# Four graph layers on one core: the order of column chunks in the attention layers

## The chip, the cores and the metric

The kernel runs on one core of a Trainium2 chip. The metric is the device time of one execution in microseconds (us). A difference between two kernels is one of the medians of repeated runs.

## The reference

A graph of 2708 nodes has an adjacency of zeros and ones, about 16 neighbours a node, and features of 512 numbers. Four layers follow each other, each with a residual and a layer norm:

```python
x = layernorm(x + relu((a_norm @ x + x) @ W0 + b0))          # layer 0
x = layernorm(x + a_norm1 @ x @ W1.T + b1)                   # layer 1
# layer 2: two attention layers, then the norm
for W in W_stack:                                            # h is the input of the first
    Wh, Ws = split(h @ W, 2)
    a = softmax(Wh @ Ws.T, axis=-1) * adj
    h = leaky_relu(a @ Wh + h, 0.01)
x = layernorm(x + h)
x = layernorm(x + adj @ (x @ W3) + b3)                       # layer 3
```

The softmax goes over all 2708 nodes; only its products with the neighbours are used.

## The kernel before

The text calls the two attention layers "layer 0 and layer 1" of the attention, as the code does, and the other layers the graph layers 0, 1 and 3. Nodes are handled in 22 blocks of 128 rows, the last with 20. The columns of the adjacency's transpose are cut into six chunks, `CH`: four of 512, one of 384 (blocks 16 to 18) and one of 276 (blocks 19 to 21). Source blocks are grouped in `GROUPS`, of 4, 4, 4, 4, 3 and 3.

A graph layer runs over steps (chunk k, group g). In each, `multiply` adds the products of a group's rows with the group's bytes of the mask into four accumulators. Rows are split in a high and a low half (`halve`: ACT makes `xh`, DVE makes `xl`), so a product appears twice, as `acc<-m,xh` and `acc<-m,xl`. The mask bytes `at` are loaded two steps ahead on SP's queue (`load_bytes`), and ACT casts them into `m`.

An attention layer first projects (`project_steps`): `wst` per chunk, and `z` per block, which is written to a scratch tensor in memory, `pairs`, in two slots that chunks use in turn. Then `layer` takes the chunks one after the other:

- `scores`: 22 matmul groups (`sp<-xs,wst_sb`) fill a chunk's columns for all source blocks; ACT copies them to `s`, DVE keeps the greatest (`top`).
- `shift_rows` and `shift_columns` make the maximum of each column (`tr_top`, `tr_mx` on PE).
- `soften`: 22 tiles, each with a subtraction (`s<-s,shift`), an exponential on ACT, a running sum (`sum<-sum,s`) and a product with the mask (`s<-s,a`). SP stores the tile beside z's rows into `pairs`.
- `fetch`: POOL gathers from `pairs`, by lists of neighbours (`givers`), 12 indirect transfers for a full block, 3 for the block of 20 rows. So a chunk of 512 has 48, that of 384 has 36 and that of 276 has 27. Eleven buffers hold them.
- `weigh`: PE multiplies each gathered tile into the result (`acc<-g`), and `end` adds the residual (`xr<-acc,rden,xr`). In layer 1 it also gathers statistics, and `normalize` writes the rows that graph layer 3 starts from (`made`).

These stages overlap: while chunk k is scored, chunk k-1 is softened and gathered, and chunk k-2 is weighed. The order of instructions on every engine is written out when the program is built (class `Ordered`, whose line is 71 in all rows of the profile). A clock that is only modelled decides there where a weighing is placed (`advance`, `until`, and 1.15 us for a gather); on the chip each engine follows that order and waits on semaphores. What fills PE after the last scores is a generator: the projections of layer 1 (`second`) after layer 0, and the first steps of graph layer 3 (`early`) after layer 1.

`early` takes 12 steps, groups 0 to 3 of chunks 0 to 2. Ahead of a step it makes sure that the rows it needs exist. `need(i)` places all weighing that is still missing for block i, in order, whether its gathers are expected or not:

```python
if t < 2:
    self.attention.need(GROUPS[t + 2][1] - 1)    # blocks 8 to 11, then 12 to 15
...
if t == 4 * TWO - 1:                             # the twelfth step
    self.attention.need(GROUPS[4][1] - 1)        # blocks 16 to 18
```

Groups 4 and 5 of the first chunks follow after the attention is done. The functions that the change touches are these:

Of the kernel before, what the change touches and what calls it, by code (L numbers as in the profile page):

```python
# [19 lines left out]
P = 128  # L20
N = 2708
D = 512
# [3 lines left out]
BANK = 512  # L26

CH = [(0, 512), (512, 512), (1024, 512), (1536, 512), (2048, 384), (2432, 276)]

GROUPS = [(0, 4), (4, 8), (8, 12), (12, 16), (16, 19), (19, 22)]  # L30
GW = 256
# [484 lines left out]
class Fast:  # L516
# [17 lines left out]
    def run(self):  # L534
        kernel, nc = self.k, self.nc
        with ExitStack() as ctx:
            pool = lambda name, bufs, **kw: ctx.enter_context(
                self.tc.tile_pool(name=name, bufs=bufs, reuse_waits="tile", **kw)
            )
            self.pages, self.wides = pool("pages", PAGES), pool("wides", WIDES)  # L540
            self.small, self.lists = pool("small_f", 4), pool("lists", 1)
            self.banks = [pool(f"banks{h}", 4, space=PSUM) for h in range(2)]
            given = [kernel.x_in[bass.ts(i, P), :] for i in range(NB)]
            l0 = Layer(0, given, kernel.w0, kernel.b0)
            l1 = Layer(1, kernel.saved[0], kernel.w1, kernel.b1)
            l3 = Layer(3, kernel.saved[2], kernel.w3, kernel.b3)
            self.attention = attention = Attention(self)
            self.jobs, self.due, self.other, self.beats = [], None, 1, 0
            run = Run(l0, l1)
            for t in range(len(run.seq)):  # L550
                self.step(run, t)
            attention.project(attention.layers[0], 0)
            for g in range(3):
                self.ends(run, g)
                if g == 1:
                    attention.project(attention.layers[0], 1)


            run = Run(l3)
            run.seq = [(l3, k, g) for k in range(TWO) for g in range(4)]  # L560
            run.seq += [(l3, k, g) for g in (4, 5) for k in range(2)]
            run.seq += [(l3, k, g) for k in range(2, TWO) for g in (4, 5)]
            run.seq += [(l3, k, g) for k in range(TWO, len(CH)) for g in range(len(GROUPS))]
            attention.run(self.early(run))
            for j in range(*GROUPS[5]):
                l3.rows[j] = attention.made[j]
            for t in range(4 * TWO, len(run.seq)):
                self.step(run, t)

            ly, k = run.before  # L570
            parts = self.project(ly, k)
            for some in (parts[:-1], parts[-1:]):
                made = []
                for i, n, ps in some:
                    made.append((i, n, self.combine(ly, k, len(made), i, n, ps)))
                self.finish(ly, k, made)
# [185 lines left out]
    def load(self, ly, k, g):  # L762

        c0, cw = CH[k]
        if (k, g) in ly.loaded:
            return
        ly.loaded.add((k, g))
        js = range(*GROUPS[g])
        if ly.number == 0:
            tiles = []  # L770
            for j in js:
                if k == 0:
                    self.load_rows(ly, j)
                at = self.wide(f"at{ly.number}_{k}_{j}")
                tiles.append(at)
                if j < NB - 1:
                    self.nc.sync.dma_start(
                        at[:, :cw], self.k.adj_t[bass.ts(j, P), c0 : c0 + cw]
                    )
                    continue  # L780

                few = self.k.adj_t[j * P : j * P + QW, c0 : c0 + cw]
                for d in range(DC):
                    self.nc.sync.dma_start(at[d * QW : (d + 1) * QW, :cw], few)
            ly.done["at", k, g] = tiles
        else:
            self.load_bytes(ly, k, g)
        if k == 0 and ly.number == 3 and g < 4:
            for j in range(*GROUPS[g]):
                self.load_rows(ly, j)  # L790
        if ly.number == 0 and g == (2 if k else 4):
            xt = [self.page(f"xt{k}_{c}") for c in range(DC)]
            for c in range(DC):
                self.nc.gpsimd.dma_start(xt[c][:, :cw], self.k.x_t[:, c, c0 : c0 + cw])
            ly.done["xt", k] = xt
# [318 lines left out]
    def step(self, run, t):  # L1114

        ly, k, g = run.seq[t]
        self.other = (k + 1) % 2
        self.before_products(run, t)
        if ly.number == 0 and (k, g) == (1, 0):
            self.attention.blank()  # L1120
        if ly.number == 1 and k == len(CH) - 1 and g in (2, 3, 4):
            self.attention.begin(g - 2)
        self.multiply(ly, k, g)
        if g == len(GROUPS) - 1 and k in ly.begun:
            self.evict(ly, k)
        wide = CH[k][1] == BANK
        if run.before and run.phase in ((1, 3, 4, 5) if wide else (1, 5)):
            self.work("PE")
        if run.before:
            self.ends(run, run.phase)  # L1130
            run.phase += 1
            if run.phase in ((3, 4, 5) if wide else (4,)):
                self.work("DVE")
        if g == (4 if ly.number == 3 and k < TWO else 3):
            self.residual(ly, k)
        if g == len(GROUPS) - 1:
            if ly.number == 3:
                self.biased(ly, k)
            if ly.number == 0:
                ends = self.degree_ends(ly, k)  # L1140
                next(ends)
                if k == len(CH) - 1:
                    note = self.prepare(
                        *run.seq[t + 1], between=lambda: next(ends), late=True
                    )
                for _ in ends:
                    pass
            while run.before and run.phase < 2:
                self.ends(run, run.phase)
                run.phase += 1  # L1150
            if k in ly.acc:
                self.evict(ly, k)
            if ly.number == 0:
                self.checked()
            run.before, run.phase = (ly, k), 0
            if ly.number == 0 and k == len(CH) - 1:
                note()
                self.load_weights(run.layers[1])
            if ly.number == 1:
                self.jobs.append((k, self.index(k)))  # L1160
                self.work("DVE")
# [178 lines left out]
class Chunk:  # L1340


    def __init__(self, ly, k):
        self.ly, self.k, self.cw = ly, k, CH[k][1]
        self.name = f"{ly.number}_{k}"
        self.blocks = blocks_of(k)
        self.s, self.masks, self.ends = {}, {}, []
        self.softened = 0
        self.fetched, self.rden = [], None
# [17 lines left out]
class Attention:  # L1367
# [29 lines left out]
    def blank(self):  # L1397
# [3 lines left out]
        for pairs in (p for ly in self.pairs for p in ly):  # L1401
            self.nc.sync.dma_start(
                pairs[N:, : 2 * PAIR + D].rearrange("j (r d) -> j r d", d=D),
                t[:n, :].unsqueeze(1).to_broadcast([n, (2 * PAIR + D) // D, D]),
            )

    def begin(self, step):

# [196 lines left out]
    def soften(self, ch):  # L1605
# [2 lines left out]
        nc, v, cw = self.nc, ch.softened, ch.cw  # L1608
        ch.softened += 1
        if v < NB:  # L1610
            if v == 0 and ch.k >= 2:

                assert not self.chunks[ch.k - 2].to_fetch
            n = rows_of(v)
            s = ch.s[v][:n, :cw]
            nc.vector.tensor_sub(s, s, ch.shift[:n, :cw])
# [9 lines left out]
        else:  # L1626
            nc.vector.tensor_add(ch.sum[:n, :cw], ch.sum[:n, :cw], s)
        nc.vector.tensor_mul(s, s, ch.masks.pop(j)[:n, :cw])
        to = ch.ly.pairs[ch.k % 2][j * P : j * P + n, :]
        if cw == BANK:  # L1630
            nc.sync.dma_start(
                to[:, : 2 * PAIR].rearrange("j (r x) -> j r x", x=PAIR)[:, :, D:],
# [26 lines left out]
    def fetch(self, ch):  # L1659
# [5 lines left out]
        if q not in ch.x:  # L1665
# [9 lines left out]
        self.nc.gpsimd.indirect_dma_start(  # L1675
            out=g[:, :width],
            out_offset=None,
            in_=ch.ly.pairs[ch.k % 2][:, :],
            in_offset=bass.IndirectOffsetOnAxis(ap=self.k.givers[:, i, t : t + 1], axis=0),
            element_offset=(q // 2) * PAIR + first,  # L1680
        )
# [103 lines left out]
    def run(self, next_layer):  # L1785

        f = self.f
        f.other = 1
        chunks = [[Chunk(ly, k) for k in range(len(CH))] for ly in self.layers]
        for k in range(2, len(CH)):  # L1790
            self.load_xt(self.layers[0], k)
            self.load_xt(self.layers[0], k + 1)
# [8 lines left out]
    def layer(self, ly, chunks, fill):  # L1801
        f = self.f
        self.chunks, self.made = chunks, {}
        for k, ch in enumerate(chunks):
# [4 lines left out]
            for n, j in enumerate(js):  # L1809
# [9 lines left out]
                self.scores(ch, j)  # L1819
                f.beat()  # L1820
                if n == 14 and k:
                    f.packed(k - 1)
                if n == 4 and k + 1 < len(chunks):
                    self.load_moving(chunks[k + 1])
                if k + 1 == len(chunks) and n in ((5, 11, 19) if ly.number == 0 else (5, 11)):
# [24 lines left out]
        done = self.clock + (2 if ly.number == 0 else 4)  # L1850
        while last.softened <= NB:
            self.soften(last)
            done += 1.4
            self.until(done, fill)
        while any(c.to_weigh for c in chunks):
            if not self.weigh() and not next(fill, False):
# [19 lines left out]
    def second(self, first):  # L1876
# [4 lines left out]
        yield True  # L1881
        self.load_w(ly)
        yield True
        self.load_xt(ly, 0)
        yield True
        yield from mixing
        for k in range(len(CH)):
            if k + 1 == len(CH) - 1:
                while self.pending:
                    self.pending.pop(0)[1]()  # L1890
                self.load_moving(first)
            if k + 1 < len(CH):
                self.load_xt(ly, k + 1)
            yield from self.project_steps(ly, k)


# [63 lines left out]
```

## Time and profile before

| | |
|---|---|
| time, median of 3 runs | 2307.89 us (2305.75 to 2312.35) |
| the profiled execution: time, and its span | 2333.96 us, 2332.2 us |
| busy PE, DVE, POOL, ACT | 2281.0, 1408.7, 705.9, 675.3 us |
| gathers (`g<-pairs,givers`) | 510, 1029 ns each on POOL |
| scores (`sp<-xs,wst_sb`, 512 columns) | 1344 matmuls of 594 ns |
| early and other products of graph layers, 512 columns | 1008 with `xh`, 1008 with `xl`, of 405 and 394 ns |
| DMA | 486.34 MB, mean 209 GB/s |

The profile is one execution, with times from the start of the span. Matmuls are pipelined, so the duration of one is longer than the distance between two: products of 512 columns start 0.23 us apart, matmuls of 512 columns in f32 are two passes in the trace. A row of a timeline has its start, its duration, the engine and line, the operation with the tiles it writes and reads, and in brackets the engine's idle time before it with what ended it. The word `issue` means that the profile shows no releaser.

### The profile page before, as it was taken

What the parts mean: (1) busy time and instruction counts of PE and PEld (TensorE: products, weight loads), DVE (VectorE), ACT (ScalarE), POOL (GpSimd) and SP (SyncE); (2) the same over time, 40 slices, a digit from 0 to 9 for tenths busy, and PEclk for the clock granted to TensorE, in tenths of its full rate; (3) what the DMA queues carried; (4) which work ended last, traced back from release to release, by engine and by line L of the source; (5) the groups of instructions that cost most, each with busy time, mean ns of one, the idle gap of its engine ahead of it and who ended that gap; (6) DMA issues with size and microseconds to landing.
All of it is one profiled execution on the core that took longest, in us unless ns stands there. A gap on an engine that the chain in (4) does not pass through costs nothing.

```text
span 2332.2 us, 25904 instructions
## 1 busy us (share of the span) xinstructions
PE 2281.0 (98%) x8525; PEld 1291.3 (55%) x8525; DVE 1408.7 (60%) x2803; ACT 675.3 (29%) x1354; POOL 705.9 (30%) x822
## 2 busy tenths in 40 slices
PE   9999999999999999999999999999999998899997
PEld 6676777777645444343555444444343454466685
DVE  6777886787554446857666511247868777534523
ACT  7444352222111123222222200123233233342221
POOL 3333431111000002534556540001634556442000
PEclk9999999999999999999999999999999999999999
DMA  9966752223557314867879997314867889873311
GB/s 349 283 186 185 186 169 79 75 79 103 205 200 267 119 45 167 309 203 276 282 268 375 326 411 301 143 41 175 291 208 270 295 284 360 270 225 117 121 50 43
DMA packets 260929, 486.34 MB, mean 209 GB/s; under 512 B 40238, under 2 KB 126950, under 8 KB 260784
## 3 DMA queue, kind: packets, MB, share of 16 engines
q1 hardware_dynamic: 192128, 269.63, 33.2%
q0 software_dynamic: 68656, 214.96, 28.2%
q8 instruction: 69, 1.13, 0.2%
q14 instruction: 76, 0.62, 0.1%
HBM read 307.55 MB, written 176.92 MB: 208 GB/s over the span
## 4 chain that ended last, share of the span: by engine, by line
PE 83%; DVE 6%; DMA 4%; issue 3%; POOL 1%; ACT 1%; another core or an unknown queue 1%; SPq 0%; POOLq 0%; DVEq 0%; ACTq 0%
PE sp L71 30%; PE acc L71 29%; PE mm L71 8%; PE z L71 6%; PE wst L71 6%; DMA g<-pairs,givers 1%; POOL g L71 1%; DVE s L71 1%; DMA at<-in_adj_t 1%; DMA x<-in_x 1%; DVE sum L71 1%; PE mix L71 1%; PE list L71 1%; PE tr_x2b L71 1%
## 5 line engine op out<-in xcount | busy, mean ns | idle before, releaser
L71 PE MATMUL sp<-xs,wst_sb 128*128 128x512 f32 (+3 forms) x2112 | 798.6, 545 | 0.4 <-issue 0.4
L71 POOL DMA_INDIRECT g<-pairs,givers x510 | 525.0, 1029 | 897.7 <-issue 399.7
L71 PEld LDWEIGHTS sp<-xs,wst_sb 128*128 128x128 f32 (+1 forms) x2112 | 379.6, 186 | 409.1 <-issue 341.8
L71 PE MATMUL acc<-m,xh 128*128 128x512 f32 (+4 forms) x1584 | 569.1, 381 | 8.4 <-ACT m L71 5.9
L71 PE MATMUL acc<-m,xl 128*128 128x512 f32 (+4 forms) x1584 | 552.1, 366 | 13.4 <-issue 10.9
L71 PEld LDWEIGHTS acc<-m,xh 128*128 128x128 f32 (+1 forms) x1584 | 289.3, 189 | 74.7 <-issue 23.6
L71 PEld LDWEIGHTS acc<-m,xl 128*128 128x128 f32 (+1 forms) x1584 | 289.6, 189 | 59.3 <-issue 17.2
L71 PE MATMUL acc<-g 128*32 128x512 f32 (+1 forms) x1020 | 268.2, 606 | 6.9 <-DMA g<-pairs,givers 3.5
L71 ACT ACTIVATE s<-s 128x512 f32<-128x512 f32 (+3 forms) x264 | 151.8, 580 | 339.6 <-DVE s L71 213.6
L71 ACT COPY s<-sp 128x512 f32<-128x512 f32 (+2 forms) x252 | 132.2, 527 | 392.8 <-PE sp L71 298.1
L71 DVE TENSOR_TENSOR top<-top,s 128x512 f32<-128x512 f32 (+2 forms) x240 | 149.4, 622 | 155.8 <-ACT s L71 123.3
L71 PE MATMUL mm<-w,ht 128*128 128x512 f32 (+1 forms) x528 | 225.0, 594 | 4.0 <-DVE ht L71 4.0
L71 ACT CAST m<-at 128x512 fp32r<-128x512 uint8 (+5 forms) x396 | 199.6, 567 | 70.0 <-DVE r L71 14.5
L71 DVE TENSOR_TENSOR s<-s,shift 128x512 f32<-128x512 f32 (+3 forms) x264 | 162.8, 620 | 38.4 <-ACT shift L71 27.3
L71 DVE TENSOR_TENSOR s<-s,a 128x512 f32<-128x512 f32 (+3 forms) x264 | 165.9, 628 | 10.0 <-issue 0.9
L71 DVE TENSOR_TENSOR sum<-sum,s 128x512 f32<-128x512 f32 (+4 forms) x252 | 156.9, 623 | 15.9 <-ACT s L71 13.6
L71 PEld LDWEIGHTS mm<-w,ht 128*128 128x128 f32 (+1 forms) x528 | 95.9, 186 | 122.6 <-issue 111.9
L71 PEld LDWEIGHTS acc<-g 128*32 128x32 f32 (+1 forms) x1020 | 75.2, 135 | 153.4 <-issue 124.5
L71 PE MATMUL z<-w,xt 128*128 128x512 f32 (+1 forms) x352 | 151.0, 596 | 0.0
L71 PE MATMUL wst<-xt,mixed 128*128 128x512 f32 (+2 forms) x384 | 150.5, 544 | 0.0
L71 POOL DMA_DIRECT2D x<-o x44 | 26.0, 597 | 353.2 <-DVE o L71 349.0
L71 DVE SCALAR_TENSOR_TENSOR xr<-acc,rden,xr 128x512 f32<-128x512 f32 (+1 forms) x44 | 32.8, 747 | 140.0 <-PE acc L71 77.5
(168 smaller groups left out, 1533.5 us busy)
## 6 DMA issues: line engine op xcount, KB each, us to landing
pairs<-z_sb SPq DMA_DIRECT2D x84, 768.0 KB
pairs<-s SPq DMA_DIRECT2D x168, 256.0 KB
at<-in_adj_t SPq DMA_DIRECT2D x84, 256.0 KB
xres<-x POOLq DMA_DIRECT2D x44, 256.0 KB
x<-o POOLq DMA_DIRECT2D x43, 256.0 KB
pairs<-s SPq DMA_DIRECT2D x84, 128.0 KB
x<-x SPq DMA_DIRECT2D x37, 256.0 KB
at<-mask SPq DMA_DIRECT2D x32, 256.0 KB
```

Of the source, the lines that this page charges most:

```text
L71: ins = call(*args, **kw)
```

## The change

Attention takes the chunks in the order 5, 0, 1, 2, 3, 4, so the chunk of 276 columns is first and that of 384 last, in both layers. A chunk's slot in `pairs` follows its place in that order. The first chunk to use slot 0 leaves 236 columns unwritten that gathers read, so these are filled with zeros once, during graph layer 1 at chunk 1, group 2. The projections of layer 1 are made in the same order. Rows of group 5 are no longer handed over in SBUF; graph layer 3 loads them as it loads those of groups 0 to 3. Those of group 4 now come from the last chunk. The modelled step of the last softening goes from 1.4 us to 0.4 us plus a share of the width.

```diff
+ORDER = (5, 0, 1, 2, 3, 4)
...
             attention.run(self.early(run))
-            for j in range(*GROUPS[5]):
-                l3.rows[j] = attention.made[j]
...
-        if k == 0 and ly.number == 3 and g < 4:
+        if k == 0 and ly.number == 3 and g != 4:
             for j in range(*GROUPS[g]):
                 self.load_rows(ly, j)
...
+        if ly.number == 1 and (k, g) == (1, 2):
+            self.attention.blank_rest()
...
-    def __init__(self, ly, k):
-        self.ly, self.k, self.cw = ly, k, CH[k][1]
+    def __init__(self, ly, at):
+        self.ly, self.at, self.k = ly, at, ORDER[at]
+        self.cw, self.slot = CH[self.k][1], at % 2
...
+    def blank_rest(self):
+        t, cw = self.page("blank_r"), CH[ORDER[0]][1]
+        self.nc.gpsimd.memset(t, 0.0)
+        at, w = PAIR + D + cw - 2 * P, 4 * P - cw
+        for ly in self.pairs:
+            for j in range(0, NB - 1, 7):
+                rows = ly[0][j * P : min(j + 7, NB - 1) * P, at : at + w]
+                self.nc.sync.dma_start(
+                    rows.rearrange("(j p) d -> p j d", p=P),
+                    t[:, :w].unsqueeze(1).to_broadcast([P, rows.shape[0] // P, w]),
+                )
+            few = N - (NB - 1) * P
+            self.nc.sync.dma_start(ly[0][N - few : N, at : at + w], t[:few, :w])
...
-        to = ch.ly.pairs[ch.k % 2][j * P : j * P + n, :]
+        to = ch.ly.pairs[ch.slot][j * P : j * P + n, :]
...
-        chunks = [[Chunk(ly, k) for k in range(len(CH))] for ly in self.layers]
+        chunks = [[Chunk(ly, at) for at in range(len(CH))] for ly in self.layers]
...
-            done += 1.4
+            done += 0.4 + last.cw / 276
...
-        self.load_xt(ly, 0)
+        self.load_xt(ly, ORDER[0])
...
-        for k in range(len(CH)):
-            if k + 1 == len(CH) - 1:
+        for at, k in enumerate(ORDER):
+            if at + 1 == len(CH) - 1:
...
-            if k + 1 < len(CH):
-                self.load_xt(ly, k + 1)
+            if at + 1 < len(CH):
+                self.load_xt(ly, ORDER[at + 1])
             yield from self.project_steps(ly, k)
```

More of the change, by code (lines that the diff above doesn't have):

```diff
@@ L1340 @@
 class Chunk:
-    def __init__(self, ly, k):
-        self.ly, self.k, self.cw = ly, k, CH[k][1]
-        self.name = f"{ly.number}_{k}"
-        self.blocks = blocks_of(k)
+    def __init__(self, ly, at):
+        self.ly, self.at, self.k = ly, at, ORDER[at]
+        self.cw, self.slot = CH[self.k][1], at % 2
+        self.name = f"{ly.number}_{self.k}"
+        self.blocks = blocks_of(self.k)
         self.s, self.masks, self.ends = {}, {}, []
@@ L1610, in soften @@
         if v < NB:
-            if v == 0 and ch.k >= 2:
-                assert not self.chunks[ch.k - 2].to_fetch
+            if v == 0 and ch.at >= 2:
+                assert not self.chunks[ch.at - 2].to_fetch
             n = rows_of(v)
@@ L1677, in fetch @@
             out_offset=None,
-            in_=ch.ly.pairs[ch.k % 2][:, :],
+            in_=ch.ly.pairs[ch.slot][:, :],
             in_offset=bass.IndirectOffsetOnAxis(ap=self.k.givers[:, i, t : t + 1], axis=0),
@@ L1821, in layer @@
                 if n == 14 and k:
-                    f.packed(k - 1)
+                    f.packed(old.k)
                 if n == 4 and k + 1 < len(chunks):
```

## The prediction

> **What bounds the kernel now.** I read the page's busy shares first, then the windows cut by stage, then the timelines of the engines around the one stage in which PE is not full. The profiled execution lasted 2333.96 us (span 2332.2 and 1.8 around it), 26 us above the median of the shown runs, 2307.89. My sums are differences inside that execution, added to the median unchanged.
>
> ```profile
> PE 2281.0 (98%) x8525; PEld 1291.3 (55%) x8525; DVE 1408.7 (60%) x2803; ACT 675.3 (29%) x1354; POOL 705.9 (30%) x822
> PE acc L71 <- issue: 14.4, 13, 9.9
> ```
>
> PE is the bound, and the change gives it the same matmuls. All it can move is the 51 us in which PE stands (2332.2 less 2281.0) and stretches in which it runs slower than it could. The windows show where those are (columns: us; busy us and instructions of PE, PEld, DVE, ACT, POOL; granted clock; DMA share; GB/s):
>
> ```profile
> 1907.00:1961.00 54.00, 53.45 (x233) 33.68 (x234) 49.78 (x107) 18.37 (x42) 34.51 (x32) 1.00 0.92 318
> 1961.00:2005.00 44.00, 32.47 (x107) 13.79 (x100) 13.66 (x28) 13.72 (x26) 26.71 (x28) 0.88 0.99 350
> 2005.00:2046.00 41.00, 31.84 (x110) 22.69 (x109) 30.95 (x75) 18.45 (x37) 11.97 (x14) 0.88 0.73 226
> 2046.00:2125.00 79.00, 79.00 (x345) 51.95 (x344) 23.46 (x51) 24.67 (x47) 38.33 (x41) 1.00 0.68 210
> ```
>
> The first row is the last scoring stage of layer 1 (276 columns), with the softening of 384 columns on DVE beside it, 49.8 of 54 us. The next two are the seam to layer 3: 20.7 us of PE idle, and a lower clock. Their cause stands in the timelines (start, duration, instruction, idle before it and its releaser):
>
> ```profile
> 1895.24 0.95 POOL L71 DMA_INDIRECT g<-pairs,givers  x1 [5.71 <-DMA a<-mask]
> 1904.89 0.49 PE L71 MATMUL tr_top<-ident,top 128*128 128x128 f32 x3
> 1970.26 0.75 DVE L71 SCALAR_TENSOR_TENSOR xr<-acc,rden,xr 128x512 f32<-128x512 f32 x1 [8.60 <-issue]
> 1974.41 0.79 PE L71 MATMUL acc<-m,xl 128*128 128x512 f32 x1 [9.92 <-issue]
> 2009.88 0.75 DVE L71 SCALAR_TENSOR_TENSOR xr<-acc,rden,xr 128x512 f32<-128x512 f32 x1 [15.80 <-remote]
> 2018.97 0.44 DVE L71 TENSOR_TENSOR s<-s,shift 128x276 f32<-128x276 f32 x1
> 2031.79 0.50 PE L71 MATMUL acc<-m,xh 128*128 128x512 f32 x1 [3.07 <-ACT m L71]
> ```
>
> DVE stood 8.6 and 15.8 us for row loads of the residual, issued some 18 to 28 us earlier on SP's queue, at a DMA share of 0.99. Behind it in DVE's order stood the halving of layer 3's rows, which PE waited for (9.92), and the softening of the last chunk. The latter's second tile comes only at 2018.97, 58 us after the last score.
>
> **What the Trainium skill says.** "DMA: Bandwidth & Descriptors", section "Issuing engines are not separate DMA queues": transfers started by SP and by GpSimd interleave on the same 16 DMA engines. The trace agrees: loads from SP's queue are late while POOL's gathers keep the share at 0.99. "PSUM — Partial Sum Buffer", section "Engine vs sequencer instructions": VectorE, ScalarE and GpSimdE take instructions strictly in order, and matmuls run in program order. The trace agrees (DVE busy 13.66 of 44 us, with softening ready but queued). "TensorE: Matmul & The Clock Gate", section "What's actually happening": an idle window of about 3.4 us halves PE's clock, as long again to return. After the wait of 9.92 us products start 0.43 us apart, later 0.23.
>
> **The change, part by part.** The built order of instructions, engine by engine, was read for both kernels (called the list below). PE and DVE carry the same number of rows; SP has 8 more DMAs for zeros, POOL one memset.
>
> (a) *Earlier stages.* The stage of 276 columns beside softening of 384 leaves both layers. In layer 0 the waits of PE between 1180 and 1273 us sum to 5.2 us (1.02, 2.02, 0.71, 0.39, 0.16, 0.91). Its successor, 384 beside 512, stands in the profile already (1840 to 1905, 0.65 idle). Layer 0's seam has 150 us of projections to cover the last chunk, gathered at the model's times, with no forced wait in the list, so 36 gathers instead of 27 are hidden there. I take a gain of 3 us, bounds 0 and 6.
>
> (b) *Zeros.* 2 x 2708 rows x 236 columns x 4 B = 5.1 MB; at 350 GB/s (20 to 60 us) some 15 us on SP's queue. The next mask bytes of layer 1's product stand behind them; such bytes are asked for two steps ahead, about 18 us. The share is 0.04 to 0.57 there. Cost 1 us, bounds 0 and 6; the memset (blank took 0.59) is hidden.
>
> (c) *Layer 1's seam.* Call T0 the end of the last scores. Layer 3's second early step calls `need(15)`, and blocks 12 to 15 are chunk 3. Before, chunk 3 was third from the end, and its weighing ran under the scores of 276 columns. Now it is second from the end: the list puts all its 48 gathers' matmuls after T0, with only one early step (32 products, 7.3 us at 0.23) among them. PE must wait for real gathers.
> - The first gather leaves 9.7 us before T0 (1904.9 less 1895.2, same widths). POOL's pitch without a wait is 1.256 us (1987.45, 1988.70, 1989.96): 48 take 60 us. The last lands some 3.5 us after issue (12th of chunk 4 out at 1995.3, used by 1998): the forced stretch ends at T0+54. PE has 22.9 us of weighing (4 blocks, each 4 x 0.93 + 2 x 1.0), 7.3 of products and 1 of transposes, so it stands 23 us.
> - DVE's list puts the four residual ends of chunk 3, its normalizing and four halvings before the second tile of chunk 4's softening. In the present seam this took 14 us (2005.2 to 2019.0): softening starts at T0+68. The halvings of rows 12 to 15 stand after 11 more tiles; a tile of 384 costs DVE 0.47 + 0.58 + 0.48 = 1.53 us (1940 to 1952): T0+85, with the first halving T0+86.5. PE has meanwhile only groups 1 and 2 of the early product, 64 x 0.23 = 15 us: it stands again, about 17 us.
> - From there PE has 288 products (65.5 us), 3 blocks of weighing (17.2) and 0.4 of sums: 83 us. The same stretch before held 86.5 by these prices and took 93.5 (2031.8 to 2125.3); with the same 7 us lost, 90: T0+176.5.
> - Chunk 4's gathers do not end later: softening ends near T0+107, the first gather 5.9 us after it (as 1889.4 to 1895.2), the 36th at T0+157. That is under PE's own order.
> - New: rows 16 to 18 come from the last chunk and are needed at once after 32 products (7.3 us). Their end, root, normalizing and halving cost 3.1 + 1.5 + 0.9 + 1.5 + 1.3 = 8.3 us and a table load; I take 2 us. Before, the last rows had two more steps of cover. Rows 19 to 21 now come by three loads asked for two steps ahead (10 us) at a share below 0.4: hidden.
>
> The seam ends at T0+178.5. Before, it ran from 1960.6 to 2125.3 = 164.7 us. After T0 PE has 3.9 us more than before (weighing 40.1 against 36.2), so T0 lies that much earlier, at 1956.7, and with (a) at 1953.7. The end of the seam moves to 2132.2, **6.9 us later**. With (b) 8 us: 2307.9 + 8 = 2316, or 0.35%. A difference of 0.3%, 7 us, is about what a measurement of this kernel can tell from no change.
>
> **The rivals.**
> *Slower by much more.* In the forced stretch, gathers (some 316 KB each) at 1.256 us are 250 GB/s, and masks, rows and residuals add about 8.7 MB in 60 us, 145 GB/s: 395 together, where the highest rate in the profile is 413. If gathers go at 1.42 us (as 1925 to 1947 beside stores) the stretch ends 8 us later. If a residual row also lands 15 us late, as at 2009.88, softening moves with it. That gives +16 to +30: 2324 to 2338. Against it: no stores of softened tiles run in that stretch.
>
> *Faster.* The row loads of chunk 3 are asked for early in the list, around T0+5 to T0+20, and with no stores beside them land before their weighing ends. Then the chain from last weighing to softening is only the arithmetic, 3.1 + 1.5 + 2.0 + 2.5 = 9 us in place of 14. If weighing also ends at T0+52, softening starts at T0+61, 7 us earlier, and all after it. The clock then halves less often, 2 us, and (a) pays its full 6. The sum is 8 - 7 - 2 - 3 - 1 = -5, to -9 if the 7 us lost later shrink too: 2299 to 2303. It decides from a start of softening under T0+61.
>
> *The gap is the same.* The two seams cost alike, since the present one loses about 45 us too and the new stalls (23 + 17) replace it: within 7 us. This is the middle of the faster case and mine. That the order isn't what the diff says is excluded by the lists.
>
> **How the numbers follow.** Mine (+5 to +14) 0.45; much slower 0.20; alike 0.22; faster 0.13. The range takes -6 to +29: 2302 to 2337. My own case and the slower rival straddle the 7 us line: slower 0.57, within 0.3% 0.29, faster 0.14.
>
> **What would show it.** Right: PE waits on gathers right after the last scores, 15 to 30 us; a second stop before the products of rows 12 to 15; the second tile of softening 60 to 75 us after the last score; no new idle in layer 0. Wrong: full PE from the last scores on, softening under 61 us, or idle at layer 0's seam or beside the zeros.

## The result, and the profile after

The change makes the kernel slower: 2348.39 us (median of 4 runs, 2348.02 to 2349.99) against 2306.98 (4 runs of the kernel before), a ratio of 1.0173 (95%: 1.0161 to 1.0186). That is 41 us, where 8 were forecast and 30 were the end of the range.

On the chips of this comparison and of the third group of experiments the kernel before takes 2307 to 2309 us, on those of the three other groups 2326 to 2327 us, so kernels are compared only within a group. The profile of before in the prediction lasted 2334 us and is nearer to the second kind.

The profiled execution of the changed kernel took 2348.02 us, its span is 2346.0. From its page, and its list of waits on PE (engine, line, what it waited for: us in total, times, longest):

```profile
PE 2289.6 (98%) x8525; PEld 1293.5 (55%) x8525; DVE 1410.9 (60%) x2803; ACT 678.8 (29%) x1356; POOL 706.4 (30%) x823
PE acc L75 <- ACT m L75: 18.5, 5, 11.2
PE acc L75 <- DMA g<-pairs,givers: 12.5, 20, 2.3
PE list L75 <- DVE both L75: 3.8, 3, 2.2
```

In the profile before, the first two kinds were 5.9 and 3.5 us. The seam by windows (columns as in the prediction). The last scores end at 1955.5, which is T0 here:

```profile
1890.00:1956.40 66.40, 65.04 (x233) 31.84 (x231) 58.67 (x101) 19.19 (x37) 42.71 (x41) 1.00 0.99 352
1956.40:2018.00 61.60, 52.30 (x133) 16.53 (x134) 19.01 (x37) 12.96 (x22) 43.97 (x45) 0.94 0.89 317
2018.00:2045.00 27.00, 15.79 (x67) 11.86 (x65) 25.23 (x53) 12.59 (x24) 2.74 (x5) 0.85 0.56 181
2045.00:2139.00 94.00, 89.83 (x366) 61.23 (x366) 32.00 (x64) 33.99 (x66) 37.13 (x40) 0.97 0.65 210
```

The second row is the forced weighing: POOL is the busy engine (43.97 of 61.6 us, 45 instructions), DVE has 19 us of work, and PE does 133 matmuls where the last row shows 366 in 94 us. The third row turns this round: DVE has the softening (25.2 of 27 us), POOL stands, and PE stands for 11.2 us. The timelines of POOL, PE and DVE give the points to which the prediction had put times:

```profile
1952.16 1.02 POOL L75 DMA_INDIRECT g<-pairs,givers  x1 [9.63 <-DMA a<-mask]
1958.57 2.05 PE L75 MATMUL acc<-g 128*128 128x512 f32 x2 [2.33 <-DMA g<-pairs,givers]
1989.34 0.75 DVE L75 SCALAR_TENSOR_TENSOR xr<-acc,rden,xr 128x512 f32<-128x512 f32 x1 [8.01 <-PE acc L75]
2013.77 0.95 POOL L75 DMA_INDIRECT g<-pairs,givers  x1 [0.30 <-PE acc L75]
2018.72 0.75 DVE L75 SCALAR_TENSOR_TENSOR xr<-acc,rden,xr 128x512 f32<-128x512 f32 x1 [11.96 <-PE acc L75]
2027.60 0.56 DVE L75 TENSOR_TENSOR s<-s,shift 128x384 f32<-128x384 f32 x1
2044.90 0.80 PE L75 MATMUL acc<-m,xh 128*128 128x512 f32 x1 [11.21 <-ACT m L75]
2068.05 1.00 POOL L75 DMA_INDIRECT g<-pairs,givers  x1 [24.27 <-issue]
```

Chunk 3's gathers run from 1952.16 to 2013.77; DVE's residual ends wait for the weighing of each block (8.0, 11.1 and, for the last, 12.0 us); only then, at 2027.60, comes the second tile of the last softening; the products of rows 12 to 15 start at 2044.90, and the last chunk's first gather leaves at 2068.05, 112.6 us after T0. So the chain that the prediction described is the one on the chip. Its lengths, and what is lost outside of it, have to be found out.

### The profile page after: what moved, and what is told of

Its sections match the earlier page's. It is cut to its first block, busy times and chain, and to the rows that moved or that the text cites. A ratio compares the mean times of both kernels' runs of the same rounds, so it can differ in the third digit from the quotient of the medians.

```text
span 2346.0 us, 25929 instructions
## 1 busy us (share of the span) xinstructions
PE 2289.6 (98%) x8525; PEld 1293.5 (55%) x8525; DVE 1410.9 (60%) x2803; ACT 678.8 (29%) x1356; POOL 706.4 (30%) x823
## 4 chain that ended last, share of the span: by engine, by line
PE 81%; DMA 7%; issue 5%; DVE 4%; ACT 1%; POOL 1%; SPq 1%; POOLq 0%; ACTq 0%; DVEq 0%
PE sp L75 32%; PE acc L75 27%; PE mm L75 7%; PE wst L75 6%; PE z L75 6%; DMA g<-pairs,givers 3%; DMA at<-in_adj_t 1%; DMA mask<-some 1%; SPq L75 1%; DVE s L75 1%; PE mix L75 1%; ACT m L75 1%; DMA at<-mask 1%; DMA x<-in_x 1%; PE list L75 0%
## 5 line engine op out<-in xcount | busy, mean ns | idle before, releaser
L75 PE MATMUL acc<-m,xh 128*128 128x512 f32 (+4 forms) x1584 | 566.7, 380 | 21.4 <-ACT m L75 18.5
L75 PE MATMUL acc<-g 128*32 128x512 f32 (+2 forms) x1020 | 280.0, 609 | 13.1 <-DMA g<-pairs,givers 12.5
L75 PEld LDWEIGHTS acc<-g 128*32 128x32 f32 (+2 forms) x1020 | 77.3, 135 | 182.1 <-issue 130.0
L75 PEld LDWEIGHTS wst<-xt,mixed 128*128 128x128 f32 x384 | 72.0, 190 | 72.7 <-issue 61.4
```

The lines of the kernel that those rows point to most:

```text
L75: ins = call(*args, **kw)
```

## The experiments

### Where the time is lost: one layer at a time

`ORDERS` gives each attention layer an order of its own. `b_again` is the kernel before, `b_zero` is that with the zeros only, `l0_only` has the new order in layer 0 and the old one in layer 1, `l1_only` the reverse, both with the zeros.

```diff
-ORDER = (5, 0, 1, 2, 3, 4)
+ORDERS = ((5, 0, 1, 2, 3, 4), (0, 1, 2, 3, 4, 5))     # l0_only
+ORDERS = ((0, 1, 2, 3, 4, 5), (5, 0, 1, 2, 3, 4))     # l1_only
...
-        self.ly, self.at, self.k = ly, at, ORDER[at]
+        self.ly, self.at, self.k = ly, at, ORDERS[ly.number][at]
```

> The kernel before, unchanged, profiled a second time. Theory A (the profile shown of before was of an execution 26 us longer than the timed ones, and the difference lies in layer 1's seam, where DVE stood 8.6 and 15.8 us for row loads): its time is 2306 and the profile's span near 2304, with the stretch from the last score to the start of the last groups' products (164.7 us in the first profile) near 140. Theory B (the extra 26 us are spread over the span, or are the price of profiling): the seam still takes about 165 us and the time outside of it is what differs.

> The kernel before plus the zeros alone (eight more transfers on SP's queue and one memset, in graph layer 1 at chunk 1, group 2). Theory A (the zeros hold up the mask bytes queued behind them, as the wait of 4.51 us in the profile of after says): slower than before by 5 us, 2311. Theory B (the wait is only moved): within 2 us of before.

> The new order in attention layer 0 alone, with the zeros; layer 1 keeps the old order and hands over the rows of group 5 as before. Theory A (the loss sits in layer 1's seam): zeros plus some 0 to 6 us less in layer 0's stages, 2305 to 2313. Theory B (layer 0 loses too, by late projections or DMA traffic): 2320 or more.

> The new order in attention layer 1 alone, with the zeros; layer 0 keeps the old order. Theory A (the forced weighing of the last chunk but one at the seam costs all): 2345 to 2350, as after. Theory B (the loss needs both layers): well under 2340.

Measured against the kernel before (2326.82 us in this group):

| kernel | median, us | ratio (95%) |
|---|---|---|
| `b_again` | 2333.42 | 1.0022 (0.9995 to 1.0049) |
| `b_zero` | 2332.86 | 1.0010 (0.9985 to 1.0035) |
| `l0_only` | 2340.39 | 1.0054 (1.0034 to 1.0073) |
| `l1_only` | 2365.63 | 1.0142 (1.0091 to 1.0194) |

The ratio is not the quotient of the two medians and differs from it most for `l1_only` (1.0142 against 1.0167). Most of the loss is layer 1's: `l1_only` is 33 us above `b_zero`, which has the same zeros and the old order. Layer 0 with the zeros loses about 0.5%; the forecast had a small gain there. Of the zeros alone the interval says only that they cost under 8 us.

### The same stretches in both kernels, on one chip

`b_third` and `a_again` are the two kernels unchanged, in one group.

> The kernel before, unchanged, for its profile beside the others of this group. Its profile shown so far lasted 2332 us, 26 us more than its timed runs. If that surplus came from the row loads that came late in layer 1's seam, a profile of a run of 2306 us shows a seam of some 130 us from the last score to the last weighing; if it came from the chip, this profile is again 2318 to 2335 us long, with a seam of 150 to 161 us.

> The changed kernel, unchanged, beside the kernel before in one group. If the change costs the same wherever it runs: 30 to 42 us over before, whatever before's own time is. If its seam is set by its gathers' pace alone while before's seam varies: 2345 to 2352 us again, and so only 15 to 25 us over before where before takes 2327 us.

Measured: before 2325.68 us, `b_third` 2328.72 (ratio 1.0017, 0.9996 to 1.0039), `a_again` 2362.65 (1.0162, 1.0129 to 1.0195). The change costs the same part on both kinds of chip, 37 us here. The base of the forecast, which put differences from a slower execution on a faster median, is therefore not what failed. The points at which the two profiles are cut behind the scores are these (`b_third`, then `a_again`; in each the last scores and the first product after layer 3's early steps, where the seam ends):

```profile
1953.10 3.99 PE L71 MATMUL sp<-xs,wst_sb 128*128 128x276 f32 x16
2117.43 0.39 PE L71 MATMUL acc<-m,xh 128*128 128x512 f32 x1
```

```profile
1959.50 5.43 PE L75 MATMUL sp<-xs,wst_sb 128*128 128x384 f32 x16
2150.23 0.50 PE L75 MATMUL acc<-m,xh 128*128 128x512 f32 x1 [1.57 <-ACT begun L75]
```

So T0 is 1957.1 in the first and 1964.9 in the second. Cut at the same events, the two profiled spans differ so (us):

| stretch | forecast | `b_third` | `a_again` | difference |
|---|---|---|---|---|
| start to the first score | +1 | 767.3 | 771.5 | +4.2 |
| to layer 1's first score | -3 | 704.5 | 710.3 | +5.8 |
| to T0, the end of the last scores | -3.9 | 485.3 | 483.1 | -2.2 |
| seam | +13.8 | 160.3 | 185.3 | **+25.0** |
| rest | 0 | 207.0 | 207.1 | +0.1 |
| span | +7.9 | 2324.4 | 2357.3 | +32.9 |

Each column is one execution. Other profiles give the seam 156.6 us (`b_again`) and 157.4 (`b_fourth`) for the kernel before, and 183.6 for the first profile of the changed one. The span of `b_again` is 7 us shorter than that of the profile in the prediction, and its seam 8 us.

### What makes the seam longer: chunk 3 late, or 384 columns last

Two orders of layer 1 take the features of the new one apart; layer 0 is as before, without zeros. Chunk 3 last but one is `(0, 1, 2, 4, 3, 5)`, `c3_late`; 384 columns last with chunk 3 in its old place is `(0, 1, 2, 3, 5, 4)`, `last_384`.

```diff
-ORDERS = ((0, 1, 2, 3, 4, 5), (5, 0, 1, 2, 3, 4))
+ORDERS = ((0, 1, 2, 3, 4, 5), (0, 1, 2, 4, 3, 5))     # c3_late
+ORDERS = ((0, 1, 2, 3, 4, 5), (0, 1, 2, 3, 5, 4))     # last_384
```

> Layer 1's attention in the order 0, 1, 2, 4, 3, 5; layer 0's as before; no zeros. The narrow chunk is still last, and chunk 3, which feeds rows 12 to 15, is now the last but one. Theory A (the second early step asks for rows 12 to 15, so TensorE weighs chunk 3 at the pace of its gathers): 20 to 30 us over before. Theory B (the seam is longer because the last chunk has 384 columns to soften and to gather): 0 to 5 us over before. Both at half: 10 to 18.

> Layer 1's attention in the order 0, 1, 2, 3, 5, 4; layer 0's as before; no zeros. The chunk of 384 columns is last, and chunk 3 keeps its place before the last two. Theory A (rows 12 to 15 asked for before chunk 3 is gathered): 0 to 5 us over before. Theory B (384 columns last): 20 to 30 us over before.

Measured in the group of `b_third`: `c3_late` 2345.72 us, ratio 1.0085 (1.0052 to 1.0118); `last_384` 2338.65, 1.0057 (1.0036 to 1.0077). The first, 20 us over before, lies at the lower edge of its theory A, the second, 13 us over, between its theories. The profiles add that either order also loses ahead of T0, which comes at 1967.1 and 1968.2 instead of 1957.1, with new waits of scores on ACT (`sp` for `s`, 2 to 3 us each). From T0 to the end of the span `c3_late` takes 377.0 us, `last_384` 368.5, `b_third` 367.3 and `a_again` 392.4. So by these profiles 384 columns last cost the seam about 1 us alone and chunk 3 late about 10; together they cost 25. (This stretch takes 363.7 to 371.5 us in four profiles of the kernel before, so the 1 and the 10 are uncertain by some 4 us.) With chunk 3 late, the last tile of softening starts 112.6 us after T0 in `c3_late` and 107.9 in `a_again`, against 84.2 in `b_third`; behind that the last gather leaves after 51 us for 276 columns and after 63 for 384.

### Moving the softening, and the zeros

If the delayed softening is the harm, it should help to emit one tile of it after each forced weighing (`a_soft`, and `b_soft` on the kernel before). `z_pool` sends the zeros by POOL's queue.

```diff
         while i not in self.made:
+            if self.last and self.last.softened <= NB:
+                self.soften(self.last)
+                self.lag = 20
             if not self.weigh(True):
...
+        self.last = last if ly.number == 1 else None
...
-        begin = max(self.fetch_free, self.clock + (16 if (q, t) == ch.first_fetch else 0))
+        begin = max(self.fetch_free, self.clock + (16 + self.lag if (q, t) == ch.first_fetch else 0))
...
-            self.nc.sync.dma_start(ly[0][N - few : N, at : at + w], t[:few, :w])
+            self.nc.gpsimd.dma_start(ly[0][N - few : N, at : at + w], t[:few, :w])   # z_pool, and the other one
```

> The changed kernel, but in layer 1 the softening of the last chunk is spread among the forced weighings of chunk 3 instead of behind them (one tile after each), and the model counts 20 us more before the last chunk's first gather. Theory A (VectorE's order: softening stands behind the residual ends that wait for chunk 3's gathers, so the last chunk's gathers start 50 us late, and rows 12 to 15 stand behind softening again): softening ends by 65 us after the last score instead of 112, the wait of 11 us before the products of rows 12 to 15 goes, 15 to 30 us faster than the changed kernel, so 5 to 20 us over before. Rival B (TensorE loses only because the 48 gathers of chunk 3 run at 1.26 us each, whoever softens when): the forced stretch stays or grows by the added work on VectorE, within 8 us of the changed kernel, 30 us or more over before.

> The kernel before with the same edit: in layer 1 the last chunk's softening is spread among the forced weighings. Theory A: before's seam loses some to the same order (second tile 52 us after the last score), so 0 to 12 us faster than before. Rival B: no gain, or a loss of up to 10 us, since before's forced weighings are mostly gathered already and softening now delays its residual ends.

> The changed kernel with the eight DMAs of zeros on POOL's queue instead of SP's. Theory A (mask bytes stand behind the zeros on SP's queue): the wait of 4 us before a product near 407 us goes and the first score comes near 768 us as in before, 4 to 6 us faster than the changed kernel. Rival B (the zeros take the DMA engines' time, whatever queue starts them): the wait stays or moves, within 2 us of the changed kernel.

Measured against 2309.47 us of before: `a_soft` 2356.47, ratio 1.0198 (1.0181 to 1.0215), `b_soft` 2321.54, 1.0058 (1.0041 to 1.0074), `z_pool` 2350.29, 1.0178 (1.0161 to 1.0195). My theory of the softening falls. Its last tile did start 72 us after T0 instead of 107, and the wait of 11 us before rows 12 to 15 is gone, yet the time is no better than the changed kernel's 1.0173. On the kernel before, the same edit costs 0.6%. The waits of PE in `a_soft`:

```profile
PE acc L75 <- DMA g<-pairs,givers: 25.3, 19, 8.4
PE acc L75 <- ACT m L75: 6.8, 4, 5.0
```

Against the first profile of the changed kernel the wait for `m` is 12 us smaller and that for gathers 13 us larger: the stall changed its name. PE's order still holds weighings ahead of gathers that haven't landed.

The zeros: in the changed kernel a product waits for mask bytes behind them, in `z_pool` it does not (first the changed kernel, with SP's issues and ACT's cast, then `z_pool`; in each PE's wait at this place and the first score).

```profile
380.73 12.75 SPq L75 DMA_DIRECT2D pairs<-blank_r  x8
393.65 10.51 SPq L75 DMA_DIRECT2D at<-mask  x5
406.76 1.66 ACT L75 CAST m<-at 128x512 fp32r<-128x512 uint8 x3 [14.73 <-DMA at<-mask]
408.48 0.80 PE L75 MATMUL acc<-m,xh 32*128 32x512 f32 x4 [4.51 <-ACT m L75]
773.12 3.27 PE L75 MATMUL sp<-xs,wst_sb 128*128 128x276 f32 x13
```

```profile
407.92 0.72 PE L75 MATMUL list<-both,at_row 128*128 128x24 bf16 x22 [1.10 <-DVE both L75]
766.51 5.83 PE L75 MATMUL sp<-xs,wst_sb 128*128 128x276 f32 x24
```

So the place behind the zeros on SP, not the bytes, causes this wait: the eight zeros alone occupy SP's issuing from 380.7 to 393.5, and the mask loads are issued after that. In `z_pool` the first score comes 6.6 us earlier. The end doesn't: from the last normalized tile to the end of the span `z_pool` takes 14 us where the changed kernel takes 7.5, and in the last 6.4 of them the profile shows neither an instruction nor a DMA. What fills them is open.

### Taking the demand away

Last, the demand itself. In `g3_after` the early steps cover groups 0 to 2 of three chunks, so that rows 12 to 15 are asked for ahead of the eighth step instead of the second; group 3 follows after the attention. `g3w_after` covers groups 0 to 2 of four chunks, which has the 12 steps and 384 products of the changed kernel again, and asks ahead of the eleventh. `g3w_before` is the same edit on the kernel before. The accumulators are parked after group 2 instead of 3. Rows 16 to 18 are handed over after the attention, so the early steps don't ask for them any more: the edit moves two demands at once.

```diff
-TWO = 3
+TWO = 4                                               # the two g3w kernels
...
-            run.seq = [(l3, k, g) for k in range(TWO) for g in range(4)]
-            run.seq += [(l3, k, g) for g in (4, 5) for k in range(2)]
-            run.seq += [(l3, k, g) for k in range(2, TWO) for g in (4, 5)]
+            run.seq = [(l3, k, g) for k in range(TWO) for g in range(3)]
+            run.seq += [(l3, k, g) for g in (3, 4, 5) for k in range(2)]
+            run.seq += [(l3, k, g) for k in range(2, TWO) for g in (3, 4, 5)]
...
-            if t < 2:
-                self.attention.need(GROUPS[t + 2][1] - 1)
+            if t in (0, 3 * TWO - 2):
+                self.attention.need(GROUPS[3 if t else 2][1] - 1)
...
-            if t == 4 * TWO - 1:
-                self.attention.need(GROUPS[4][1] - 1)
-                for j in range(*GROUPS[4]):
-                    ly.rows[j] = self.attention.made[j]
```

> The kernel before, unchanged, for a profile on the chip of this group. Where its timed runs take 2306 to 2310 us: last score near 1948 us and a seam (last score to last weighing) of 150 to 155 us, so that the changed kernel's seam of 174.5 plus 7.4 us of products that it has after the last weighing is the larger by some 30 us, and its last score by some 8. Where they take 2325 us: 1957 to 1960 us and 154 to 159 us again.

> The changed kernel, but the early steps of graph layer 3 cover groups 0 to 2 only (9 steps, 288 products instead of 384), so that rows 12 to 15 are asked for seven steps later; group 3 of the first three chunks follows after the attention. Theory A (asking for rows 12 to 15 right after the last scores makes TensorE weigh chunk 3 at the gathers' pace, and delays the last softening): 20 to 35 us faster than the changed kernel, 5 to 20 us over before or less. Rival C (the seam lasts as long as the gathers of 84 tiles and the last softening take, whatever TensorE does meanwhile; with 96 products fewer it only waits more): no gain, or up to 10 us slower than the changed kernel.

> The same as g3_after, with groups 0 to 2 of four chunks early (12 steps, 384 products as in the changed kernel). Theory A: 20 to 40 us faster than the changed kernel, and no slower than g3_after. Rival C: at the changed kernel's time within 8 us, and 5 to 15 us faster than g3_after since it has more to do while it waits.

> The kernel before with the same edit as g3w_after (groups 0 to 2 of four chunks early). Theory A: before loses less to this demand, since chunk 3's gathers are mostly done at the last score; 0 to 15 us faster than before. If g3w_after comes down to this kernel's time within 10 us, the demand for rows 12 to 15 holds nearly the whole of the change's loss. Rival C: no gain over before, and g3w_after 25 us or more above this one.

Measured against 2326.70 us of before:

| kernel | median, us | ratio (95%) |
|---|---|---|
| `b_fourth` (before, unchanged) | 2325.49 | 0.9991 (0.9973 to 1.0010) |
| `g3_after` | 2342.62 | 1.0062 (1.0044 to 1.0080) |
| `g3w_after` | 2326.71 | 0.9991 (0.9979 to 1.0003) |
| `g3w_before` | 2315.44 | 0.9941 (0.9924 to 0.9959) |

The new order with the demand moved takes what the kernel before takes. The page and the waits of `g3w_after`, to be read against those of the changed kernel:

```profile
PE 2277.3 (98%) x8525; PEld 1292.7 (56%) x8525; DVE 1415.5 (61%) x2805; ACT 678.5 (29%) x1356; POOL 706.5 (30%) x823
PE acc L75 <- ACT m L75: 5.0, 2, 3.9
PE acc L75 <- DMA g<-pairs,givers: 3.8, 5, 1.5
```

The wait for `m` fell from 18.5 to 5.0 us and that for gathers from 12.5 to 3.8. PE's busy time fell from 2289.6 to 2277.3 us for the same matmuls. It shows in the weighing (busy, mean ns of one, idle before it and what ended it); first the changed kernel in the group of `b_third` (`a_again`), then `g3w_after`:

```profile
L75 PE MATMUL acc<-g 128*32 128x512 f32 (+2 forms) x1020 | 285.9, 610 | 18.7 <-DMA g<-pairs,givers 10.1 <-issue 4.2 <-DVE rden L75 3.1
```

```profile
L75 PE MATMUL acc<-g 128*32 128x512 f32 (+2 forms) x1020 | 268.7, 608 | 16.2 <-issue 5.8 <-DVE rden L75 5.3 <-DMA g<-pairs,givers 3.8
```

The same 1020 matmuls, as long one by one, keep PE busy 17 us longer in the changed kernel, so they overlap less there. I read this as more waiting for gathers, which the list of waits doesn't show; in `b_third` the weighing takes 266.9 us. The softening in `g3w_after` (its second tile, and the last scores before it):

```profile
1964.23 5.43 PE L75 MATMUL sp<-xs,wst_sb 128*128 128x384 f32 x16
2000.24 0.56 DVE L75 TENSOR_TENSOR s<-s,shift 128x384 f32<-128x384 f32 x1
```

The second tile comes 30.6 us after T0 instead of 72. Rival C is half right: `g3_after` has the demand away but 96 products fewer to fill the seam, and takes 16 us more than `g3w_after`. `g3w_before` is faster than both kernels of this case, by 0.6% than before: the kernel before paid for the demands too, only less. That it is rows 12 to 15 and not 16 to 18 is argued, not tested alone: at the end of the early steps of the changed kernel PE waits 1.6 us only, and `last_384`, which also takes rows 16 to 18 from its last chunk in the twelfth step, has about the seam of before.

## Why the prediction was wrong

**The account.** On the slower chips the order costs 37.0 us with the demands in place (2362.65 less 2325.68). With them moved in both kernels it costs 11.3 (2326.71 less 2315.44, in another group). So some 26 us of the change go through them, uncertain by about 9 as the intervals combine, and 11 us lie elsewhere. The stretches agree: the seam is 25.0 us longer, all else 7.9. The prediction had put 13.8 on the seam, -3.9 on T0 and -2 on what comes before layer 1. Its direction and the mechanism of the seam were right, and the terms were mis-sized in three places; for layer 0 the sign was wrong too.

**The seam's new length.** "The first gather leaves 9.7 us before T0" is the step that failed first. That was measured at another pair of stages, and then T0 alone was moved forward by the weighing that left it; the gathers were not moved against it. In fact softening took what it had taken (57.3 us from first to last tile in both stages), T0 came closer to its end (15.1 us after the start of the last tile in place of 18.8), and the gather left 11.7 us after that start, not 9.1. It left 3.3 us before T0 in the changed kernel's first profile and 4.7 in `a_again`. What follows (us after T0):

| event | forecast | first profile | `a_again` |
|---|---|---|---|
| last gather of chunk 3 leaves | 49.4 | 58.3 | 58.9 |
| forced weighing ends | 54 | 63.2 | 63.7 |
| second tile of softening | 68 | 72.1 | 73.1 |
| products of rows 12 to 15 | 86.5 | 89.4 | 90.3 |
| early steps done, next product | 178.5 | 183.6 | 185.3 |

The forced stretch is 9 us longer than forecast: 6.4 of them in the first profile are the later start, the rest is a pitch of 1.31 us a gather in place of 1.256. From its end to the second tile of softening 9 us pass, not the 14 that were taken from the profile before, and so half of the loss comes back; the stop "about 17 us" was 11.2. The rival "slower by much more" had priced a forced stretch 8 us longer, at 0.20, and its length came true. Its reason did not: the gathers did not go at 1.42 us each, and no residual row was late in the first profile, where chunk 3's residual ends wait for PE alone. (The 413 GB/s quoted there as the highest rate is 411 on the page of before.) The chain of 9 us had been the argument of the rival "faster". At the place of the two us for rows 16 to 18 PE waits 1.6, which the profile puts to the parking of the accumulators (`begun`).

**The seam's old length.** The 164.7 us came from one execution, with DVE waits of 8.6 and 15.8 us, read as residual rows that landed late, and PE's 9.92. In `b_third` and `b_fourth` PE's longest wait for `issue` is 2.4 and 4.4 us, and the seam is 160.3 and 157.4. So 4 to 8 us of what was subtracted belonged to that execution: "the present one loses about 45 us too" held for that profile, not for the kernel. The new length is short by 5 to 7 us and the old one long by 4 to 8; together this is the seam's miss of 11 us (25.0 against 13.8).

**The zeros and layer 0.** (b) at 1 us and (a) at a gain of 3 us make -2 us together, where the runs with the demands moved leave +11. Every profile with the zeros on SP's queue has its first score at 771.5 to 776.4 us, against 767 to 769 without: about 5 us (2 to 9), where my bounds were 0 to 6 and my value 1. I had the mask bytes behind the zeros in the text and priced the delay away by the two steps of notice. The timed runs are too unsteady to show this cost: `b_zero` takes 2332.86 us and `b_again` 2333.42. The Trainium skill, "TensorE: Matmul & The Clock Gate", section "What's actually happening", says that PE's clock is halved after an idle window of about 3.4 us, and full again only after about as long at work. The profile agrees: after this wait of 4.5 us the granted clock of the 20 us from 400 on is 0.83, in before's profile 1.00, so the stop costs more than its length. In layer 0 the old waits that I wanted to save are gone, but new ones take their place: in `l0_only` one weighing waits 4.79 us for `rden`, and the lists wait 3.8 us on DVE where before has 1.7. But `b_zero` and `l1_only`, with the zeros and the old order in layer 0, take 709.2 and 710.6 us from the first score to layer 1's, about as long as the 710.3 of `a_again` and more than the 704.5 of `b_third`. So the +5.8 can't be put to layer 0's order alone. How the 11 us divide is not settled.

**Right.** Little idle beside the last scores (PE 65.0 of 66.4 us); PE waits on gathers directly after T0 (the list of waits has 12.5 us, where 15 to 30 were expected); a second stop before rows 12 to 15; the second tile of softening at 72.1 us (60 to 75); no wait of PE or DVE for the loads of rows 19 to 21; the last softening is done 109.8 us after T0 (forecast 107), and the first gather behind it leaves at 112.6.

## What to carry to other kernels

When an order of production is changed, look first for the consumer that asks by position in a fixed order: here such demands, by all signs the call for rows 12 to 15, made some 26 of the 37 us that a reorder cost, and asking later, with as much other work in between, gave them back. The stall that `a_soft` moved inside a fixed order of PE came back under another name, so try to remove the demand, not the wait. Take the base of a difference from more than one profile wherever it holds waits on DMA.

## What was not expected of the hardware

The kernel before takes 2307 to 2309 us in two of the five groups of runs and about 2326 in the others, which ran on other chips. In the latter its runs spread widely (2316 to 2333 in 19 runs beside `a_again`, 2318 to 2337 in 39 runs beside `g3w_after`), while the four runs of `a_again` lie within 5 us; four runs are few, and those of `l1_only` spread over 10. Why is open. The eight zeros occupied SP's issuing for 12.8 us and so held up the mask loads behind them. Sent by POOL's queue they took away a wait of 4.5 us, yet in the one profile of that kernel the stretch after the last visible instruction is 14 us instead of 7.5.
